# Layer 0 sums taken beside the heads' sums, and layer 0 logits spread by on-chip transfers, in a two-layer graph attention kernel

## The chip, the cores and the metric

The kernel runs on one core of a Trainium2 chip. The core has TensorE (PE, matrix products), VectorE (DVE), ScalarE (ACT), GpSimd (POOL) and SyncE (SP, which here issues nearly all transfers). The metric is device time in microseconds for one execution. All arithmetic is in 32 bit floats.

## The reference

x holds 64 graphs of 256 nodes with 512 features; adj is one 256 x 256 adjacency matrix for all of them. Two attention layers follow one another. Both normalize, clip at zero, attend along the edges and add the result to x.

```python
# layer 0: one head, additive logits
h = relu(layernorm(x))
Wh = h @ W
logits = (Wh @ a_src)[:, :, None] + (Wh @ a_dst)[:, None, :]
logits = where(logits >= 0, logits, 0.2 * logits)
attn = softmax(where(adj == 0, -inf, logits), axis=-1)
x = x + attn @ Wh
# layer 1: eight heads of 64, dot products
h = relu(layernorm(x))
q, k, v = (split_heads(h @ W.T + b) for W, b in ((Wq, bq), (Wk, bk), (Wv, bv)))
attn = softmax(where(adj == 0, -inf, q @ k.T / 8), axis=-1)
x = x + merge_heads(attn @ v) @ Wo.T + bo
```

## The kernel before

**One graph at a time, many graphs in flight.** A graph is 256 tokens, kept as two tiles of 128 partitions (P = 128, NT = NC = 2). The work on a graph is cut into stages, each a Python generator. A loop over i runs a list of steps, `first_half + second_half`; each entry is a stage with an offset, so that one pass works on graphs i - 2 to i + 3. Every engine executes its instructions in the order in which the steps emit them. This hand-written order is the whole schedule. A tile name that is used with one buffer makes its next writer wait for its last reader.

**Short names in the lists.** D0 and N0 are normalize0 (of graphs i + 2 and i + 3), E0 weights0, Q0 quarters0, U0 and US aggregate0, W transform0, N1 and X1 the normalization and transposition of layer 1, K project_qk, V project_v, A and A_OLD attention, AS and AS_OLD scale, O output, BO bias_rows. The large products (K, V, W, O, and the seven small ones of U0) use a Strassen-like scheme of seven half-size products; the sums that it needs (hs, us, as, hq, eq) are made by POOL in `combine`, and DVE adds the products up.

**Layer 0, in order.** normalize0 makes h on ACT and, as its last step (D0), the logits es and ed of the nodes on DVE: four products with accumulation (L511), one column per tile of tokens. weights0 (E0) has three steps. The first spreads es along partitions with two PE transposes into a PSUM bank, pe (L525), from which ACT takes four exponentials (L532, L533). The second takes their maximum on DVE (L537), multiplies it with the mask (em, L540) and adds the two halves up (esum, L542), both on POOL. The third adds esum over partitions with a PE product with ones (ps, L556); DVE clips it (L558) and takes the reciprocal of all 256 columns, the same on all 128 partitions (L559), into the tile rb0. quarters0 (Q0) multiplies em by rb0 on POOL (L578) and makes the differences eq (L588). aggregate0 multiplies h with em (pu, L606).

**Layer 1, the part concerned.** attention takes six steps: the scores of all heads into eight PSUM banks (psc, L838) with exponentials on ACT (L846); four steps of masks and row sums on DVE (L851, L853); and a last step with the products with v (pav, L863) and head_sums. That adds the sums of the eight heads up over partitions with eight PE products on 32-column tiles of the array (psm, L878), so that each head has 16 partitions, and takes one reciprocal of 256 columns (rc, L886). Eight transfers by SP (rb, L909) then spread each head's row over 64 partitions, and scale multiplies aT by rb on DVE (L936) ahead of output. For the last two graphs products with `pick` do it instead of transfers.

**Which graphs.** PLAIN = 3: from graph 3 on, layer 0 goes through quarters0 and the seven small products. PSUM has eight banks, all handed out from one pool by `bank`.

**Around it.** A second path, general, runs only when a test of the weights' size fails; it isn't executed here.

Of the kernel before, what the change touches and what calls it, by code (L numbers as in the profile page):

```python
# [9 lines left out]
F32 = mybir.dt.float32  # L10
# [6 lines left out]
P = 128  # L17
# [6 lines left out]
Q = 32  # L24
# [4 lines left out]
def kernel(  # L29
# [26 lines left out]
    nc = tc.nc  # L56
    B, N, D = x.shape
    NC = N // P
    DC = D // P
    NT = GB * NC  # L60
    TOK = NT * P
    G = B // GB
    DH = D // HEADS
# [16 lines left out]
    ident = const.tile([P, P], F32, tag="ident", name="ident")  # L80
    make_identity(nc, ident)
    ones = const.tile([P, P], F32, tag="ones", name="ones")
# [49 lines left out]
    def bounded():  # L132
        weights = ctx_b.enter_context(tc.tile_pool(name="weights", bufs=1))
        big = ctx_b.enter_context(tc.tile_pool(name="big", bufs=1))
        work = ctx_b.enter_context(tc.tile_pool(name="work", bufs=1))
# [3 lines left out]
        def bank(shape, name):  # L139
            return ps_mm.tile(shape, F32, tag="mm", name=name)  # L140
# [207 lines left out]
        pick = weights.tile([P, P], F32, tag="pick", name="pick")  # L348
# [10 lines left out]
        def constants():  # L359

            ok = weights.tile([P, 2 * DC + 5], F32, tag="ok", name="ok")
            rows = weights.tile([P, 2 * DC], F32, tag="rows", name="rows")
            gms = []
            for n in range(2):
                w_q = whole((wq_sb, wk_sb)[n])  # L370

                gm = work.tile([P, DC, DH], F32, tag="gram", name=f"gram_{n}", bufs=2)
                gms.append(gm)
                for pair in range(2):
                    pg = bank([P, 2, DH], f"pgram_{n}_{pair}")
                    for e in range(2):
                        for c in range(DC):
                            for r in range(2):
                                at = e * P + r * DH
                                wc = w_q[c // 2][pair][:, c % 2, at : at + DH]  # L380
                                nc.tensor.matmul(
                                    pg[r * DH : (r + 1) * DH, e, :], wc, wc,
                                    start=(c == 0), stop=(c == DC - 1),
                                )
                    yield
                    nc.vector.tensor_copy(gm[:, 2 * pair : 2 * pair + 2, :], pg)
                    yield
            for n, gm in enumerate(gms):
                pgs = [bank([P, DC, DH], f"pgram2_{n}_{r}") for r in range(2)]
                for e in range(DC):  # L390
                    for r in range(2):
                        half_p = slice(r * DH, (r + 1) * DH)
                        part = gm[half_p, e, :]
                        nc.tensor.matmul(pgs[r][half_p, e, :], part, part, start=True, stop=True)
                yield
                for e in range(DC):
                    for r in range(2):
                        half_p = slice(r * DH, (r + 1) * DH)
                        ab = work.tile([P, DH], F32, tag="gabs", name=f"gabs_{n}_{e}_{r}")
                        nc.scalar.activation(  # L400
                            ab[half_p], pgs[r][half_p, e, :], AF.Abs,
                            accum_out=rows[half_p, n * DC + e : n * DC + e + 1],
                        )
                yield
            for _ in range(10):
                yield
            sq = weights.tile([P, 4], F32, tag="sq", name="sq")
            for j, col in enumerate((cols["bq"], cols["bk"])):
                junk = work.tile([P, DC], F32, tag="e2", name=f"junk_c_{j}")
                nc.vector.scalar_tensor_tensor(  # L410
                    junk, col, 1.0, col, op0=ALU.mult, op1=ALU.mult, accum_out=sq[:, j : j + 1]
                )
            for _ in range(4):
                yield
            pq = bank([P, 2], "pq")
            nc.tensor.matmul(pq, ones, sq[:, 0:2], start=True, stop=True)
            yield
            nc.vector.tensor_scalar(
                ok[:, 2 * DC + 2 : 2 * DC + 4], pq, 1.0, None, op0=ALU.is_le
            )  # L420
            yield
            for j in range(2):
                junk = work.tile([P, D], F32, tag="e2", name=f"junk_w_{j}")
                nc.vector.scalar_tensor_tensor(
                    junk, wa[j], 1.0, wa[j], op0=ALU.mult, op1=ALU.mult, accum_out=sq[:, 2 + j : 3 + j]
                )
                yield
            nc.vector.tensor_scalar(ok[:, 0 : 2 * DC], rows, 1.0, None, op0=ALU.is_le)
            nc.vector.tensor_scalar(ok[:, 2 * DC : 2 * DC + 2], sq[:, 2:4], 1.95, None, op0=ALU.is_le)
            yield  # L430
            big_v = weights.tile([P, 1], F32, tag="big_v", name="big_v")
            nc.vector.tensor_reduce(big_v, svs, AX.X, ALU.add)
            nc.vector.tensor_scalar(
                ok[:, 2 * DC + 4 : 2 * DC + 5], big_v, 1.0e6, None, op0=ALU.is_le
            )
            okm = weights.tile([P, 1], F32, tag="okm", name="okm")
            nc.vector.tensor_reduce(okm, ok, AX.X, ALU.min)
            for _ in range(12):
                yield
            pk = bank([1, 1], "pok")  # L440
            nc.tensor.matmul(pk, okm, ones[:, 0:1], start=True, stop=True)
            nc.vector.tensor_scalar(flag, pk, P - 0.5, None, op0=ALU.is_lt)
            yield
            picks()
            yield

        class Stats:

# [30 lines left out]
        nodes, edges, sums0, lefts, norms, qkv, vs, outs = {}, {}, {}, {}, {}, {}, {}, {}  # L479

        def normalize0(g):
# [26 lines left out]
            for t in range(NT):  # L508
                for dst, a in ((es, 0), (ed, 1)):
# [3 lines left out]
                        accum_out=dst[:, t : t + 1],  # L513
                    )
            nodes[g] = h, es, ed
            yield

        def weights0(g):

            h, es, ed = nodes[g]  # L520
            edl = small.tile([P, NT], F32, tag="edl", name=f"edl_{g}")
            nc.scalar.mul(edl, ed, NEG_SLOPE)
            pe = bank([P, TOK], f"pe_{g}")
            for t in range(NT):
                nc.tensor.transpose(  # L525
                    pe[:, t * P : (t + 1) * P], es[:, t : t + 1].to_broadcast([P, P]), ident
                )

            e1 = work.tile([P, NC, N], F32, tag="e1", name=f"e1_{g}")
            e2 = work.tile([P, NC, N], F32, tag="e2", name=f"e2_{g}")  # L530
# [10 lines left out]
            esum = work.tile([P, N], F32, tag="esum", name=f"esum_{g}")  # L541
            engine.tensor_tensor(esum, em[:, 0, :], em[:, 1, :], op=ALU.add)  # L542
            edges[g] = [em]
            yield

            if g == 0:
                ps = bank([P, NT], f"ps_{g}")
# [11 lines left out]
            nc.vector.reciprocal(rs, rs)  # L559
            edges[g].append(rs)  # L560
            yield


        PLAIN = 3

        def quarters0(g):

# [257 lines left out]
        def attention(g):  # L825
# [46 lines left out]

            def head_sums():

                psm = bank([P, N], f"psm_{g}")
                for r in range(2):
                    for e in range(DC):
                        nc.tensor.matmul(  # L878
                            psm[e * Q : (e + 1) * Q, :],
                            half[:, r, :],  # L880
                            sums[e][:, r, :],
                            start=(r == 0),
                            stop=(r == 1),
                        )
                rc = work.tile([P, N], F32, tag="rc", name=f"rc_{g}")
                nc.vector.reciprocal(rc, psm)  # L886
                return rc

            exs = [scores(e) for e in range(DC)]
# [14 lines left out]
            if g < G - 2:  # L904
                rb = work.tile([P, DC, N], F32, tag="rb", name=f"rb_{g}")
                for e in range(DC):
                    for r in range(2):
                        src = rc[e * Q + r * (Q // 2) : e * Q + r * (Q // 2) + 1, :]
                        nc.sync.dma_start(  # L909
                            rb[r * DH : (r + 1) * DH, e, :],  # L910
                            bass.AP(
                                tensor=src.tensor, offset=src.offset,
                                ap=[src.ap[0], [0, DH], [1, N]],
                            ),
                        )
            else:

                yield
                rb = [bank([P, N], f"prb_{g}_{e}") for e in range(DC)]
                for e in range(DC):  # L920
                    rows = slice(e * Q, (e + 1) * Q)
                    nc.tensor.matmul(rb[e], pick[rows, :], rc[rows, :], start=True, stop=True)
            outs[g] = aT, rb
            yield

# [89 lines left out]
        def aside(n=1):  # L1015
# [5 lines left out]
        Q0 = (quarters0, 2)  # L1021
# [1 line left out]
        A, A_OLD, BO = (attention, 0), (attention, -1), (bias_rows, 0)  # L1023
        AS, AS_OLD = (scale, -1), (scale, -2)
        first_half = [
            (load, 3), O, D0, K, AS_OLD, O, K, O, K, E0, O, K, E0, O, US, A_OLD, K, O, K, BO, O, K, E0,
        ]
        second_half = [
            A_OLD, A, Q0, A, W, N0, W, W, V, N0, W, W, W, N1, W, N1, A, V, V, V, A, N0, N1, U0, V, AS,
            U0, X1, V, X1, V, X1,  # L1030
        ]

# [259 lines left out]
```

## Time and profile before

| what | value |
|---|---|
| median of 2 runs | 2848.22 us (2846.7 to 2849.74) |
| the profiled execution's own time | 2846.97 us |
| its span, first to last instruction | 2845.2 us |
| PE busy | 2828.9 us (99%) |
| DVE busy | 2473.5 us (87%) |
| POOL busy | 1607.0 us (56%) |
| ACT busy | 1257.3 us (44%) |
| DMA queue of SP | 107.53 MB, 23.7% of 16 engines |
| granted PE clock | 1.00 |

The span is the time between the first and the last instruction of the profiled execution; 1.8 us of its own time lie around it. Busy time is what an engine spends in instructions. PE's records overlap, since its products are pipelined: of two products, the distance between their starts is the price, not the length of one. In a group's line the columns are source line, engine, operation, names out<-in, shapes, count, busy time, mean length in ns, and idle time of the engine ahead of it with what ended it. In a timeline line they are start and length in us, engine, line, operation, names, shapes and count of records that follow one another. A product in 32 bit floats appears as two PE records; a transpose as one.

### The profile page before, as it was taken

The numbers are of one execution on the slowest core, as the hardware profiler recorded it, in microseconds if no ns is written. First come the engines' busy times: TensorE is split into PE (matmuls) and PEld (weight loads), VectorE is DVE, ScalarE is ACT, GpSimd is POOL, SyncE is SP. The second block draws the span as 40 slices with busy tenths as digits, with TensorE's granted clock in tenths as the row PEclk, the third lists the DMA queues.
The fourth block names the chain that finished last, engine by engine and source line by source line (L and its number), as shares of the span: only waits on it lengthen the run. The fifth ranks groups of instructions, "written<-read, shape, count | busy, mean of one in ns | idle before, by whom it ended". The sixth has DMA issues, their size and how long they took to land. (4 is left out here: it accounts for less than half of the span.)

```text
span 2845.2 us, 53317 instructions
## 1 busy us (share of the span) xinstructions
PE 2828.9 (99%) x20316; PEld 2472.3 (87%) x20316; DVE 2473.5 (87%) x3946; ACT 1257.3 (44%) x3045; POOL 1607.0 (56%) x2016
## 2 busy tenths in 40 slices
PE   9999999999999999999999999999999999999998
PEld 6888988988889889888898898888988988889886
DVE  7998988888889888888898888888988888889875
ACT  5444444443444444434444444344454443444532
POOL 2656556566565565665655655656556556565541
PEclk9999999999999999999999999999999999999999
DMA  4122122221221222212212222122122221221221
GB/s 134 23 38 38 34 42 33 36 45 31 38 38 34 42 33 36 45 31 38 39 33 42 33 36 46 31 38 40 32 42 33 36 45 31 38 42 30 34 42 27
DMA packets 82826, 111.01 MB, mean 39 GB/s; under 512 B 11524, under 2 KB 48644, under 8 KB 82566
## 3 DMA queue, kind: packets, MB, share of 16 engines
q1 hardware_dynamic: 82470, 107.53, 23.7%
q8 instruction: 164, 2.69, 0.4%
q14 instruction: 96, 0.79, 0.1%
q0 software_dynamic: 96, 0.01, 0.0%
HBM read 41.43 MB, written 33.55 MB: 26 GB/s over the span
## 5 line engine op out<-in xcount | busy, mean ns | idle before, releaser
L701 DVE TENSOR_TENSOR x<-po,x 128x1024 f32<-128x1024 f32 x875 | 593.8, 685 | 130.2 <-PE po L207 122.9
L851 DVE TENSOR_TENSOR ex<-ex,maskT 128x512 f32<-128x512 f32 x512 | 435.3, 890 | 0.0
L474 POOL TENSOR_SCALAR ve<-ssq 128x2 f32<-128x2 f32 x127 | 25.1, 198 | 483.8 <-ACT h L463 250.6
L846 ACT ACTIVATE ex<-psc 128x512 f32<-128x512 f32 x512 | 257.7, 627 | 89.5 <-PE psc L838 89.4
L871 ACT COPY aT<-pav 128x512 f32<-128x512 f32 x128 | 74.9, 585 | 499.2 <-PE pav L863 468.1
L511 DVE SCALAR_TENSOR_TENSOR junk<-wa,h 128x512 f32<-128x512 f32 x252 | 276.6, 1098 | 7.9 <-ACT h L504 1.1
L216 PEld LDWEIGHTS pqk<-hs,wq_sb 128*128 128x128 f32 x2016 | 264.4, 192 | 12.9
L216 PE MATMUL pqk<-hs,wk_sb 128*128 128x128 f32 x2016 | 266.3, 275 | 0.0
L216 PE MATMUL pqk<-hs,wq_sb 128*128 128x128 f32 x2016 | 265.8, 275 | 0.0
L207 PE MATMUL pv<-wv_sb,hs 128*128 128x256 f32 x1024 | 262.9, 380 | 0.6 <-DVE v L194 0.5
L540 POOL TENSOR_TENSOR em<-e,maskT 128x512 f32<-128x512 f32 x62 | 79.6, 1283 | 321.7 <-DVE e L537 312.0
L207 PE MATMUL po<-wo_sb,as 128*128 128x256 f32 x992 | 255.2, 380 | 0.0
L207 PE MATMUL po<-w_sb,us 128*128 128x256 f32 x1008 | 248.5, 379 | 0.0
L216 PEld LDWEIGHTS pqk<-hs,wk_sb 128*128 128x128 f32 x2016 | 245.4, 192 | 0.0
L838 PE MATMUL psc<-qk 64*128 64x256 f32 x2048 | 239.0, 383 | 0.3 <-DVE rc L886 0.3
L863 PE MATMUL pav<-ex,v 128*64 128x256 f32 x2048 | 235.4, 382 | 0.0
L838 PEld LDWEIGHTS psc<-qk 64*128 64x128 f32 x2048 | 193.1, 187 | 46.9 <-issue 25.0
L165 POOL TENSOR_TENSOR hs<-hT 128x256 f32<-128x256 f32 x64 | 47.0, 735 | 319.2 <-PE pv L207 319.2
L853 DVE TENSOR_TENSOR sm<-ex 128x512 f32<-128x512 f32 x256 | 210.5, 822 | 8.9
L863 PEld LDWEIGHTS pav<-ex,v 128*64 128x64 f32 x2048 | 141.2, 137 | 85.8 <-issue 20.3
L207 PEld LDWEIGHTS po<-w_sb,us 128*128 128x128 f32 x1008 | 191.4, 190 | 26.3 <-DVE x L701 0.3
L216 PEld LDWEIGHTS pqk<-hT,wq_sb 128*128 128x128 f32 x1512 | 198.2, 192 | 9.6
(211 smaller groups left out, 6564.5 us busy)
## 6 DMA issues: line engine op xcount, KB each, us to landing
x<-in_x_dram SPq DMA_DIRECT2D x64, 512.0 KB, 5.6
out_dram<-x SPq DMA_DIRECT2D x128, 256.0 KB, 2.0
rb<-rc SPq DMA_DIRECT2D x496, 64.0 KB, 4.9
wq_sb<-in_L_gnn_Wq_dram SPq DMA_DIRECT2D x4, 256.0 KB, 8.4
wk_sb<-in_L_gnn_Wk_dram SPq DMA_DIRECT2D x4, 256.0 KB, 6.7
w_sb<-in_L_gnn_W_dram SPq DMA_DIRECT2D x4, 256.0 KB, 6.6
wv_sb<-in_L_gnn_Wv_dram SPq DMA_DIRECT2D x4, 256.0 KB, 6.6
wo_sb<-in_L_gnn_Wo_dram SPq DMA_DIRECT2D x4, 256.0 KB, 6.0
```

What stands on the lines that cost most here:

```text
L165: nc.gpsimd.tensor_tensor(s[:, 0], a(1, 0), a(1, 1), op=ALU.add)
L207: nc.tensor.matmul(dst[:, 0:HD], left[:, c, :], wt[:, slot, c, :], start=c == 0, stop=c == 1)
L216: nc.tensor.matmul(dst[:, at : at + P], wt[:, slot, c, e * P : (e + 1) * P], left[:, c, :], start=c == 0, stop=c == 1,)
L511: nc.vector.scalar_tensor_tensor(junk, (wa if g else pas)[a], 1.0, h[:, t, :], op0=ALU.mult, op1=ALU.mult, accum_out=dst[:, t : t + 1],)
L540: engine.tensor_tensor(em, e1, maskT, op=ALU.mult)
L701: nc.vector.tensor_add(dst, src, dst)
L838: nc.tensor.matmul(psc[r][:, m, :], qk[rows, 2 + e % 2, m * P : (m + 1) * P], qk[rows, e % 2, :], start=True, stop=True,)
L846: nc.scalar.activation(ex[:, r, :, :], psc[r], AF.Exp, scale=SCALE)
L851: nc.vector.tensor_mul(ex[:, r, :, :], ex[:, r, :, :], maskT)
L853: nc.vector.tensor_add(sm, ex[:, :, 0, :], ex[:, :, 1, :])
L863: nc.tensor.matmul(pav[r * DH : (r + 1) * DH, i, :], v[j][:, m, at : at + DH], pair[i][:, r, m, :], start=(m == 0), stop=(m == NC - 1),)
L871: nc.scalar.copy(aT[j], pav)
```

## The change

For graphs 3 to 63 two things are done in another way.

The row of logits es isn't transposed by PE. normalize0, in its last step, has SP write the two columns of es into one row of 256 on one partition (es_row, two transfers of 128 single elements), and then spread that row over 128 partitions (es_b). ACT's exponentials read es_b. es_row shares its buffer (tag rc) with the heads' reciprocals, es_b shares esum's.

The sum of esum isn't taken by weights0, whose third step now does nothing there. head_sums of the graph three before takes it, with four PE products of 64 columns each, ahead of its own eight and in the same PSUM bank, which is widened to 320 columns. Each quarter of the nodes lies on 32 partitions, so that the maximum and reciprocal on DVE have 64 columns. Four transfers spread the quarters into rb0, ahead of the eight that spread rb.

The order of the steps changes: the first step of E0 comes after the fourth K instead of the third; the second after the fifth K, with US, BO and A_OLD now ahead of it; the third is dropped. In the second half one V goes ahead of the first U0.

```diff
@@ normalize0
             nodes[g] = h, es, ed
+            if g >= PLAIN:
+                row = work.tile([1, TOK], F32, tag="rc", name=f"es_row_{g}")
+                for t in range(NT):
+                    nc.sync.dma_start(row[:, t * P : (t + 1) * P], es[:, t : t + 1])
+                es_b = work.tile([P, TOK], F32, tag="esum", name=f"es_b_{g}")
+                spread(es_b, row)
+                nodes[g] = h, es_b, ed
             yield
@@ new
+        def spread(dst, row):
+            nc.sync.dma_start(
+                dst,
+                bass.AP(
+                    tensor=row.tensor, offset=row.offset,
+                    ap=[row.ap[0], [0, dst.shape[0]], [1, dst.shape[1]]],
+                ),
+            )
@@ weights0
-            pe = bank([P, TOK], f"pe_{g}")
-            for t in range(NT):
-                nc.tensor.transpose(
-                    pe[:, t * P : (t + 1) * P], es[:, t : t + 1].to_broadcast([P, P]), ident
-                )
+            pe = es
+            if g < PLAIN:
+                pe = bank([P, TOK], f"pe_{g}")
...
             edges[g] = [em]
+            if g >= PLAIN:
+                edges[g].append(esum)
             yield
+            if g >= PLAIN:
+                return
@@ head_sums
-                psm = bank([P, N], f"psm_{g}")
+                psm = bank([P, N + DH], f"psm_{g}")
+                rc = work.tile([P, N + DH], F32, tag="rc", name=f"rc_{g}")
+                g0 = g + PLAIN
+                if g0 < G:
+                    part = slice(N, N + DH)
+                    for e in range(DC):
+                        rows = slice(e * Q, (e + 1) * Q)
+                        nc.tensor.matmul(
+                            psm[rows, part], ones[:, 0:Q], edges[g0][1][:, e * DH : (e + 1) * DH],
+                            start=True, stop=True,
+                        )
...
-                rc = work.tile([P, N], F32, tag="rc", name=f"rc_{g}")
-                nc.vector.reciprocal(rc, psm)
+                if g0 < G:
+                    nc.vector.tensor_scalar_max(rc[:, part], psm[:, part], 1e-38)
+                    nc.vector.reciprocal(rc[:, part], rc[:, part])
+                    rb0 = work.tile([P, N], F32, tag="rb0", name=f"rb0_{g0}")
+                    for e in range(DC):
+                        spread(rb0[:, e * DH : (e + 1) * DH], rc[e * Q : e * Q + 1, part])
+                    edges[g0][1] = rb0
+                nc.vector.reciprocal(rc[:, 0:N], psm[:, 0:N])
@@ order of the steps
-            (load, 3), O, D0, K, AS_OLD, O, K, O, K, E0, O, K, E0, O, US, A_OLD, K, O, K, BO, O, K, E0,
+            (load, 3), O, D0, K, AS_OLD, O, K, O, K, O, K, E0, O, US, BO, A_OLD, K, E0, O, K, O, K,
-            A_OLD, A, Q0, A, W, N0, W, W, V, N0, W, W, W, N1, W, N1, A, V, V, V, A, N0, N1, U0, V, AS,
+            A_OLD, A, Q0, A, W, N0, W, W, V, N0, W, W, W, N1, W, N1, A, V, V, V, A, N0, N1, V, U0, AS,
```

More of the change, by code (lines that the diff above doesn't have):

```diff
@@ L398, in constants @@
                         half_p = slice(r * DH, (r + 1) * DH)
-                        ab = work.tile([P, DH], F32, tag="gabs", name=f"gabs_{n}_{e}_{r}")
+                        ab = work.tile([P, DH], F32, tag="rc", name=f"gabs_{n}_{e}_{r}")
                         nc.scalar.activation(
@@ L445, in constants @@
             yield
+        PLAIN = 3
+        def spread(dst, row):
[6 more added lines that the diff above has]
+            )
         class Stats:
@@ L522, in weights0 @@
             nc.scalar.mul(edl, ed, NEG_SLOPE)
-            pe = bank([P, TOK], f"pe_{g}")
-            for t in range(NT):
-                nc.tensor.transpose(
-                    pe[:, t * P : (t + 1) * P], es[:, t : t + 1].to_broadcast([P, P]), ident
-                )
+            pe = es
+            if g < PLAIN:
+                pe = bank([P, TOK], f"pe_{g}")
+                for t in range(NT):
+                    nc.tensor.transpose(
+                        pe[:, t * P : (t + 1) * P], es[:, t : t + 1].to_broadcast([P, P]), ident
+                    )
             e1 = work.tile([P, NC, N], F32, tag="e1", name=f"e1_{g}")
@@ L561, in weights0 @@
             yield
-        PLAIN = 3
         def quarters0(g):
@@ L873, in head_sums @@
             def head_sums():
-                psm = bank([P, N], f"psm_{g}")
+                psm = bank([P, N + DH], f"psm_{g}")
[8 more added lines that the diff above has]
+                            start=True, stop=True,
+                        )
                 for r in range(2):
@@ L878, in head_sums @@
                         nc.tensor.matmul(
-                            psm[e * Q : (e + 1) * Q, :],
+                            psm[e * Q : (e + 1) * Q, 0:N],
                             half[:, r, :],
@@ L907, in attention @@
                     for r in range(2):
[L908 to L915, printed above, removed]
+                        at = e * Q + r * (Q // 2)
+                        spread(rb[r * DH : (r + 1) * DH, e, :], rc[at : at + 1, 0:N])
             else:
@@ L921, in attention @@
                     rows = slice(e * Q, (e + 1) * Q)
-                    nc.tensor.matmul(rb[e], pick[rows, :], rc[rows, :], start=True, stop=True)
+                    nc.tensor.matmul(rb[e], pick[rows, :], rc[rows, 0:N], start=True, stop=True)
             outs[g] = aT, rb
```

## The prediction

> **What bounds the kernel now.** I read the engine totals first, then TensorE's waits, then the PE, DVE and SP rows of one steady pass of the loop over graphs (43.74 us by the PE rows, 1430.35 to 1474.09), and last the DMA issues.
>
> ```profile
> PE 2828.9 (99%) x20316; PEld 2472.3 (87%) x20316; DVE 2473.5 (87%) x3946; ACT 1257.3 (44%) x3045; POOL 1607.0 (56%) x2016
> ...
> PE pt L750 <- ACT xn L729: 4.9, 3, 3.1
> PE pa L263 <- DMA a_in<-in_L_gnn_a_src_dram: 2.2, 1, 2.2
> PE pwa L274 <- DVE junk_a L270: 1.5, 5, 0.6
> ```
>
> PE is idle for 16.3 us of the 2845.2 us span, and its named waits (3 or 5 times each) lie in the start. In the steady pass it never waits: time is PE work. So an edit pays only by what it takes off PE, and costs only where it makes PE wait.
>
> ```profile
> 1437.40 1.06 PE L216 MATMUL pqk<-hT,wk_sb 128*128 128x128 f32 x8
> 1438.29 0.38 PE L525 MATMUL pe<-ident,es 128*128 128x128 f32 x2
> 1438.51 1.03 PE L207 MATMUL po<-wo_sb,as 128*128 128x256 f32 x4
> ...
> 1449.11 0.60 PE L556 MATMUL ps<-esum,ones 128*128 128x256 f32 x2
> 1449.64 3.67 PE L863 MATMUL pav<-ex,v 128*64 128x256 f32 x32
> 1453.24 1.07 PE L878 MATMUL psm<-sm,half 128*32 128x256 f32 x16
> ```
>
> Columns: start, length, instruction. Lengths overlap, so the price is the distance between starts. The transposes hold PE 0.22 us (1438.29 to 1438.51), the layer 0 sum 0.53 us (1449.11 to 1449.64), the sixteen records of the eight head sums only 1.00 us.
>
> [...] The trace agrees. From the last record of one mode to the first of the next it shows 309 ns where 216 is usual, a drain of 93 ns; and the sixteen 216 ns records of psm fit in 1.00 us, four abreast. [...] In the packet records the first 64 KB spread of rb, all from one partition, moves between 1.12 and 3.27 us after its issue: 30 GB/s. [...] So es_row and es_b cost two latencies in series; no run here shows such a pair yet.
>
> **The change part by part.** It acts on graphs 3 to 63, 61 of 64.
>
> Removed from PE. Two transposes, 2 x 109 = 218 ns. The ones-by-esum product is two records of 216 to 218 ns; the drain before pav (93 ns) stays, since pav then follows a 128-column record, so 434 ns go. Together 0.652 us a graph.
>
> Added to PE. Four matmuls of 64 columns on 32-column tiles, eight records, just ahead of psm in psm's own mode: no second drain. The nearest row is pgram (64 columns, two tiles): 106 ns for its first round after a change of mode, then 58 a round. Two rounds are 0.165 us; psm's first round, now not the first of its mode, falls from 240 to 216 ns. I take 0.14 us. From below: two rounds by columns alone, 2 x 54 - 24 = 0.085. From above: eight records in series at 58, about 0.5.
>
> Net 0.652 - 0.14 = 0.51 us a graph, times 61 = 31 us; with the bounds 0.57 and 0.15, or 35 and 9 us.
>
> DVE. The maximum (411 ns) and reciprocal (1753 ns) of 256 columns go, those of 64 columns come, about 0.22 and 0.5 us by scaling the two rows. 1.4 us a graph less, 89 us in all, worth nothing because DVE isn't the bound. But both now stand ahead of the heads' reciprocal, and the first waits for the whole psm. So the heads' reciprocal, which starts at 1454.38, ends some 0.7 us later, at 1456.9. In the new order the psm bank goes to the second product of transform0, at 1458.87: hidden by 2 us.
>
> DMA and SP. Seven transfers more a graph: two of es_row (128 elements of 4 B), es_b (128 KB), four of rb0 (32 KB each).
>
> ```profile
> 1447.48 2.96 SPq L957 DMA_DIRECT2D out_dram<-x  x2
> 1456.17 6.63 SPq L909 DMA_DIRECT2D rb<-rc  x8
> 1462.84 0.64 SPq L225 DMA_DIRECT2D x<-in_x_dram  x1
> ...
> out_dram<-x SPq DMA_DIRECT2D x128, 256.0 KB, 2.0
> rb<-rc SPq DMA_DIRECT2D x496, 64.0 KB, 4.9
> ```
>
> SP is idle between 1419 and 1447, where es_row and es_b come; behind them wait only the two stores, which have the x buffers as slack.
>
> Chain 1, the logits (own clock of this pass).
>
> ```profile
> 1435.98 1.09 DVE L511 SCALAR_TENSOR_TENSOR junk<-wa,h 128x512 f32<-128x512 f32 x1
> 1443.17 2.51 DVE L851 TENSOR_TENSOR ex<-ex,maskT 128x512 f32<-128x512 f32 x2
> 1445.72 1.10 DVE L853 TENSOR_TENSOR sm<-ex 128x512 f32<-128x512 f32 x1
> ...
> 1442.73 1.27 POOL L540 TENSOR_TENSOR em<-e,maskT 128x512 f32<-128x512 f32 x1 [5.08 <-DVE e L537]
> 1444.08 1.05 POOL L542 TENSOR_TENSOR esum<-em 128x256 f32<-128x256 f32 x1
> ```
>
> The second half of es is ready at 1437.1. es_row then takes 2.0 (the store, also 128 pieces) to 4.9 us (rb's median), I take 2.0. es_b reads twice the bytes of a first rb from one partition: 1.1 + 4.3 + 0.4 = 5.8 us, between 4.9 (the median) and 6.4 (rb's longest). es_b lands at 1445.0, at worst 1448.4. Who waits: ACT's four exponentials (1.57 us) and, behind them on ACT, the copies of the fifth Q/K product; DVE's maximum (0.68), put behind the mask pair that ends near 1446, and behind it six adds; POOL's em and esum (2.4). The sum must be there when PE comes to psm, 1453.24 - 0.65 = 1452.6. Backwards: em by 1450.2, the maximum by 1449.5, es_b by 1447.9. Slack 2.9 us, at worst 0.5 short. Moving us and the bias ahead of em costs nothing: POOL is through with both near 1444.5. The six adds end near 1452, and scores start after 1453.6.
>
> Chain 2, the reciprocals. rb0 is issued from 1455.1, four issues at about 0.6 us[...]. By bytes it lands some 6 us later, 1461; no row shows 256 B pieces, so the upper bound is that its 512 pieces last like rb's 512 of 1 KB: in the packet records the last rb lands 10.9 us after the first issue, 1466. POOL needs 1.4 us for em times rb0 and 1.9 for the two first differences; PE's second pu product, with the V product moved ahead of it, comes at 1468.4. rb0 must land by 1465. Then the eight rb spreads land near 1470 instead of 1467.1; the scaling of aT on DVE, before the next pass's first output product, needs the last by 1473.3. Slack 3 to 4 us in both.
>
> PSUM. Two banks fewer are taken a pass, 48 instead of 50; nothing there comes late.
>
> Sum: 2846.97 (own time of the profiled execution: span 2845.2 plus 1.8) - 31 = 2816. The median of the two runs is 1.3 us above the profiled one, less than the error here.
>
> **The rivals.**
> A. The small matmuls run one after the other. For: no row shows four tiles at 64 columns. Against: psm does four abreast. Net 0.15 us x 61 = 9 us: 2838.
> B. Slower than before: late spreads at rb. Twelve transfers leave one after the other, and O1 stands behind aT on rb. If a 256 B piece costs what a 1 KB piece does, rb0 ends at 1466, and the eight of rb, 9.8 us behind it, at 1475.8: 2.5 us past need, in each pass. PE would wait 2.5 us against 0.51 saved: 2847 + 61 x 2.0 = 2969. It decides from a landing after 1473.8. For: pieces of rb last 46 ns or 500, so they queue. Against: 30 GB/s looks like a limit of bytes, and rb0 carries a quarter of rb's.
> C. No saving: with chain 1 at its upper bounds PE waits 0.5 us at psm, which eats it: 2847. For: the 4 B pieces are new. Against: both latencies must be at their upper end.
> D. Faster by over 2%. Even free sums and no new wait give 0.652 x 61 = 40 us, 2807, and the idle time of the start isn't touched.
>
> **How the numbers follow.** Forecast 0.73, A 0.07, B 0.12 (anywhere from 2848 to 2969, two thirds of it over 2%), C 0.07, D 0.01. The likeliest is 2816. Its own range with the bounds is 2812 to 2838; the range goes to 2808 below, the end of D's arithmetic, and to 2850 above, which takes in A and C and leaves most of B out. 2% is 57 us, about what a measurement of this kernel can tell from no change: faster 0.02, same 0.90, slower 0.08.
>
> **What would show it.** Right: no pe rows and no sum rows on PE but for graphs 0 to 2; starts of the new matmuls and of the first psm record 0.14 to 0.19 us apart; a pass of 43.2 us; PE idle still near 16 us. Chain 1 is wrong if psm waits for POOL's esum, chain 2 if pu waits for POOL or po for DVE's aT. The forecast is wrong if PE's idle time grows by more than 10 us.

## The result and the profile after

| | before | after |
|---|---|---|
| median | 2848.22 us (2846.7 to 2849.74) | 2821.36 us (2820.66 to 2822.05) |
| profiled execution, own time | 2846.97 us | 2820.66 us |
| its span | 2845.2 us | 2818.9 us |
| a steady pass, distance of the starts of psm | 43.746 us | 43.205 us |
| PE idle, span minus busy | 16.3 us | 19.8 us |

The ratio after to before is 0.9903 with the interval [0.988, 0.9927]: about 1% less time, within the 2% that was called no change, and 5 us above the forecast of 2816. The steady pass gained 0.541 us; 61 passes of that are 33.0 us. The two profiled executions differ by only 26.3 us. So the pass did slightly better than forecast, and 6.7 us were lost somewhere else. Most of this section is about where.

First the engine totals of the kernel after:

```profile
PE 2799.1 (99%) x20560; PEld 2455.8 (87%) x20560; DVE 2335.3 (83%) x3946; ACT 1259.0 (45%) x3045; POOL 1502.0 (53%) x2016
```

Some of its groups (count, busy time and mean in ns, then the idle time before them and what ended it):

```profile
L876 DVE TENSOR_TENSOR ex<-ex,maskT 128x512 f32<-128x512 f32 x512 | 368.0, 759 | 0.0
L603 POOL TENSOR_TENSOR em<-em,rb 128x256 f32<-128x256 f32 x122 | 86.2, 728 | 468.7 <-DMA rb<-rc 468.7
L555 ACT ACTIVATE e<-es_b,ed 128x256 f32<-128x256 f32 x122 | 61.0, 500 | 433.9 <-DMA es_b<-es_row 433.9
```

And three of its DMA issues (count, KB each, median us from issue to landing):

```profile
es_b<-es_row SPq DMA_DIRECT2D x61, 128.0 KB, 6.4
rb<-rc SPq DMA_DIRECT2D x244, 32.0 KB, 3.8
es_row<-es SPq DMA_DIRECT2D x122, 0.5 KB, 1.9
```

PE is still busy 99% of the span. ACT and POOL now wait more than 430 us each for the new transfers (7 to 8 us a pass), and PE doesn't notice: neither engine is the bound. Those two large idle figures cost nothing, because PE's own list of waits has neither of them (total, number of times, longest):

```profile
PE pt L775 <- ACT xn L754: 4.9, 3, 3.1
PE psc L863 <- DVE qk L201: 3.3, 1, 3.3
PE pa L263 <- DMA a_in<-in_L_gnn_a_src_dram: 2.3, 1, 2.3
PE pav L888 <- ACT gabs L400: 2.0, 1, 2.0
```

The first and third were there before. The second and fourth are new, and each happens once. No wait happens 61 times: the pass runs without a stall, as before. PE's rows of one steady pass, around the added matmuls:

```profile
1400.72 0.32 PE L908 MATMUL psm<-esum,ones 128*32 128x64 f32 x8
1400.86 1.05 PE L914 MATMUL psm<-sm,half 128*32 128x256 f32 x16
1401.84 3.72 PE L863 MATMUL psc<-qk 64*128 64x256 f32 x32
...
1439.34 1.06 PE L216 MATMUL pqk<-hs,wk_sb 128*128 128x128 f32 x8
1440.33 3.67 PE L888 MATMUL pav<-ex,v 128*64 128x256 f32 x32
```

Before, pav followed the two ps records; now it follows a Q/K product directly. The heads' sums start 0.14 us after the small matmuls.

**The start is where the 6.7 us went.** The first head sums, before and then after:

```profile
95.58 1.07 PE L878 MATMUL psm<-sm,half 128*32 128x256 f32 x16
98.78 1.05 PE L914 MATMUL psm<-sm,half 128*32 128x256 f32 x16
```

They start 3.2 us later. The second ones come 44.98 us behind them before and 48.48 us after: 3.5 us. Together these two account for the loss. The rows of the kernel after in that stretch (start, length, engine and line; in brackets the idle time before it and what ended it):

```profile
90.22 0.22 ACT L400 ACTIVATE gabs<-pgram 64x64 f32<-64x64 f32 x1 [9.21 <-DMA es_b<-es_row]
...
93.36 5.36 PE L888 MATMUL pav<-ex,v 128*64 128x256 f32 x32 [2.00 <-ACT gabs L400]
99.18 1.14 ACT L823 ACTIVATE p<-pqk,bias 128x128 f32<-128x128 f32 x4
100.35 0.89 DVE L198 TENSOR_TENSOR qk<-qk,p 128x512 f32<-128x512 f32 x1 [3.97 <-ACT p L823]
103.12 1.13 PE L863 MATMUL psc<-qk 64*128 64x256 f32 x8 [3.30 <-DVE qk L201]
```

gabs is scratch of the test of the weights' size, which is made once, in the first passes of the loop. An edit that the diff above leaves out moves it into the buffer rc:

```diff
-                        ab = work.tile([P, DH], F32, tag="gabs", name=f"gabs_{n}_{e}_{r}")
+                        ab = work.tile([P, DH], F32, tag="rc", name=f"gabs_{n}_{e}_{r}")
```

es_row lies in rc too, and rc is one buffer. So the first gabs has to wait until the transfer that spreads es_row has read it, and ACT stands for 9.21 us; what its program has behind that gabs comes late with it. The sixteen gabs start between 80.2 and 88.5 us before, and between 90.2 and 98.7 us after. PE waits 2.00 us at pav, and the profile names gabs, which reads its products from PSUM, as what ended the wait. Behind the last gabs ACT gets to p, the summand of a Q/K product (99.18); DVE waits 3.97 us for it, and PE 3.30 us at psc for DVE's sum.

The 5.3 us of stalls are not the whole price. The table by windows has for the stretch 60 to 110 us (length, then busy time of PE, PEld, DVE, ACT and POOL with counts, then granted PE clock, DMA share, GB/s), first before,

```profile
60.00:110.00 50.00, 45.96 (x332) 38.42 (x331) 47.02 (x68) 29.00 (x88) 27.99 (x33) 1.00 0.15 11
```

then after:

```profile
60.00:110.00 50.00, 41.45 (x298) 34.40 (x297) 40.47 (x59) 23.84 (x72) 23.01 (x24) 0.90 0.14 7
```

The granted clock falls from 1.00 to 0.90: three windows of 3.41 us at half clock lie there, from 73.6, 94.0 and 104.3 us. The profiled execution of the kernel before has none in the start. The first window follows a stall of 3.1 us at pt that both kernels have. The other two follow the two new stalls, and in them pav takes 5.36 us, where 3.67 is usual, and psc 5.41, where 3.72 is usual. So the 6.7 us have two parts: 3.5 us are more idle time of PE (19.8 against 16.3 us), and 3.2 us are longer records (PE is busy for 2799.1 us, where 2828.9 - 33.0 = 2795.9 would be left).

### The profile page after: what moved, and what is told of

Same layout as the page of the kernel before. It is cut to its first block, busy times and chain, and to the rows that moved or that the text cites. A ratio compares the mean times of both kernels' runs of the same rounds, so it can differ in the third digit from the quotient of the medians.

```text
span 2818.9 us, 54598 instructions
## 1 busy us (share of the span) xinstructions
PE 2799.1 (99%) x20560; PEld 2455.8 (87%) x20560; DVE 2335.3 (83%) x3946; ACT 1259.0 (45%) x3045; POOL 1502.0 (53%) x2016
## 5 line engine op out<-in xcount | busy, mean ns | idle before, releaser
L876 DVE TENSOR_TENSOR ex<-ex,maskT 128x512 f32<-128x512 f32 x512 | 368.0, 759 | 0.0
L603 POOL TENSOR_TENSOR em<-em,rb 128x256 f32<-128x256 f32 x122 | 86.2, 728 | 468.7 <-DMA rb<-rc 468.7
L555 ACT ACTIVATE e<-es_b,ed 128x256 f32<-128x256 f32 x122 | 61.0, 500 | 433.9 <-DMA es_b<-es_row 433.9
L207 PE MATMUL pv<-wv_sb,hs 128*128 128x256 f32 x1024 | 253.5, 380 | 0.6 <-DVE v L194 0.5
L563 POOL TENSOR_TENSOR em<-e,maskT 128x512 f32<-128x512 f32 x62 | 79.2, 1278 | 263.8 <-DVE e L560 254.0
L207 PEld LDWEIGHTS pv<-wv_sb,hs 128*128 128x128 f32 x1024 | 190.2, 191 | 24.5 <-DVE v L194 0.9
```

The source lines that it names most:

```text
L207: nc.tensor.matmul(dst[:, 0:HD], left[:, c, :], wt[:, slot, c, :], start=c == 0, stop=c == 1)
L555: nc.scalar.activation(e1[:, m, :], pe, AF.Exp, bias=ed[:, m : m + 1])
L563: engine.tensor_tensor(em, e1, maskT, op=ALU.mult)
L603: nc.gpsimd.tensor_tensor(em[:, m, :], em[:, m, :], rb, op=ALU.mult)
L876: nc.vector.tensor_mul(ex[:, r, :, :], ex[:, r, :, :], maskT)
```

## The experiments

Where nothing else is said, an experiment starts from the version with gabs in another buffer, so that the start disturbs no comparison. Its pass is also 43.205 us.

**The change again** (no edit).

> The changed kernel once more, beside its variants. Both theories: 0.9905 of before, 2821 us; one pass of the loop over graphs 43.20 us against 43.75; the start some 7 us longer than before's.

Measured: 2820.27 us (2819.7 to 2823.28), ratio 0.9904 [0.9888, 0.9919]; pass 43.205 us. The first result stands.

**gabs in another buffer.**

```diff
-                        ab = work.tile([P, DH], F32, tag="rc", name=f"gabs_{n}_{e}_{r}")
+                        ab = work.tile([P, DH], F32, tag="s2v", name=f"gabs_{n}_{e}_{r}")
```

> The changed kernel with gabs in the buffer s2v instead of rc. Theory G (the 5 us missing from the forecast are lost at the start, because gabs shares rc with es_row and so makes ACT wait for the landing of es_b): ACT's wait of 9.2 us ahead of gabs, PE's waits of 2.0 us at pav and 3.3 us at psc and the windows of half PE clock that follow them go, 7 us less, 2814 us; the pass stays 43.20 us. Theory S (the loss comes from the order of steps and the transfers themselves, whatever buffer gabs has): the waits move to the exponentials and stay, 2821 us.

Measured: 2816.35 us (2815.08 to 2818.73), ratio 0.9893 [0.9878, 0.9908]. Repeated later:

> The kernel with gabs apart once more, beside it: 2816 us, 0.989 of before; its profile again without half clock in the start, or[...] with one or two.

Measured: 2817.44 us (2816.07 to 2818.82), ratio 0.9894 [0.9877, 0.991]. The highest of all these runs (2818.8) lies below the lowest of the change's in the repetition (2819.7), though the intervals of the ratios overlap. The gain is 4 us, where theory G expected 7. The waits for gabs and for the late Q/K sum are gone from PE's list; one new wait is left in the first pass, and here is the start of that version: its first psm row,

```profile
97.80 0.32 PE L908 MATMUL psm<-esum,ones 128*32 128x64 f32 x8 [2.73 <-POOL esum L565]
```

and its window:

```profile
60.00:110.00 50.00, 43.79 (x328) 36.80 (x327) 46.00 (x66) 27.33 (x83) 26.68 (x31) 1.00 0.20 12
```

The clock is 1.00 here, and PE does 328 records in the stretch against 298. So the buffer of gabs costs about 4 us. In the repetition the same kernel had the same stalls, but also two windows of 3.4 us at half clock in its start, and its span was 3.0 us longer (2816.3 against 2813.3 us). So these windows vary between executions, and I don't count them as caused by gabs alone. Of the 6.7 us about 4 are shown to hang on this edit. The wait for esum doesn't make up the rest: the execution without half clock has this wait too, and its span is 31.9 us below that of before, only 1.1 us short of the 33.0 us that the passes gain. What is missing beyond that goes with the half clock.

**Move what fills ACT and DVE in the start, to let that esum come earlier.** In the first pass DVE also combines the weights (combine_w). This version spreads one of these combinations over four later places:

```diff
-        def combine_w(wt):
-            for to, a, b in ((T1, T3, B11), (T2, B22, T1), (T3, B22, T3), (T4N, B21, T2)):
+        def combine_w(wt, part=slice(0, 4)):
+            for to, a, b in ((T1, T3, B11), (T2, B22, T1), (T3, B22, T3), (T4N, B21, T2))[part]:
...
-                if i == 1 and n == 9:
-                    combine_w(wo_sb)
+                if i == 1 and n in (24, 28, 32, 36):
+                    combine_w(wo_sb, slice(n // 4 - 6, n // 4 - 5))
```

> As the kernel with gabs apart, with DVE's four subtractions for the quarters of wo_sb, which stand ahead of the fourth mask in pass 1 and last 5.2 us there, put one by one into the second half of that pass. Theory (they make DVE late for the maximum, POOL for esum, and PE waits 2.7 us for it at psm in pass 1): that wait goes, 3 us less than the kernel with gabs apart, 2813 us. Rival (the subtractions cost DVE the same in the second half, where PE waits for its adds): 2816 us or more.

Measured: 2816.95 us (2816.41 to 2820.2), ratio 0.9892 [0.9876, 0.9909]: no gain over the 2817.44 us of the version with gabs apart that ran beside it. The wait for esum is gone, and PE's list has instead

```profile
PE psc L863 <- DVE qk L201: 2.7, 1, 2.7
```

A stall of the same size one product further on: in the start, taking away the wait that ends last brings up the next. The two versions can't be told apart by their times.

**The logits by transposes again, the sums as in the change.**

```diff
-            if g >= PLAIN:
-                row = work.tile([1, TOK], F32, tag="rc", name=f"es_row_{g}")
...
-                nodes[g] = h, es_b, ed
...
-            pe = es
-            if g < PLAIN:
-                pe = bank([P, TOK], f"pe_{g}")
-                for t in range(NT):
...
+            pe = bank([P, TOK], f"pe_{g}")
+            for t in range(NT):
...
```

> As the kernel with gabs apart, but the row of logits comes from the two PE transposes again; es_row and es_b are gone, the sums stay beside the heads' sums. If the price of a PE record is the distance between starts: 0.218 us a pass more, 61 x 0.218 = 13 us above the kernel with gabs apart, 2827 us, pass 43.42 us. Rival: transposes were free beside other PE work, then no difference.

Measured: 2832.27 us (2830.77 to 2832.97), ratio 0.9946 [0.9933, 0.996]; pass 43.423 us. That is 0.218 us above 43.205, the price forecast for two transposes. It divides the gain of a pass: the transfers in place of transposes are worth 0.218 us, the sums beside the heads' sums 43.746 - 43.423 = 0.323 us. In the first pass PE waits for esum here too:

```profile
PE psm L898 <- POOL esum L555: 3.1, 1, 3.1
```

No transfer stands in the path of this esum. So that wait doesn't come from the transfers; by the version with combine_w spread out, where it is gone, it comes from DVE's work in the first pass.

**The small matmuls three times.**

```diff
-                    for e in range(DC):
+                    for e in [*range(DC)] * 3:
```

> As the kernel with gabs apart, with the four small matmuls issued three times over in each pass instead of once. Theory of the forecast (four tiles abreast, 58 ns a round of four): two more sets are four rounds, 0.23 us a pass, 61 x 0.23 = 14 us, 2830 us, pass 43.44 us. Rival (one after the other): sixteen more records at 58 ns, 0.93 us a pass, 57 us, 2873 us.

Measured: 2831.16 us (2829.51 to 2832.2), ratio 0.9937 [0.9924, 0.9951]; pass 43.428 us. Its rows:

```profile
1404.44 0.54 PE L908 MATMUL psm<-esum,ones 128*32 128x64 f32 x24
1404.80 1.05 PE L914 MATMUL psm<-sm,half 128*32 128x256 f32 x16
```

24 records take 0.36 us to the start of psm, where 8 took 0.14. Two more sets cost 0.223 us, and a set is two rounds of records, so a round of four tiles costs 0.223 / 4 = 56 ns, and one record costs no more than a quarter of that. Single starts within a round lie 6 to 7 ns apart, and the next round begins 37 ns later. Had the tiles run in series, two sets would have cost 16 records of 56 ns, 0.9 us.

**The sum of 256 columns, in the place of the small matmuls.** One product with ones where the four were; DVE's maximum and reciprocal have 256 columns and write rb0, and its four transfers go.

```diff
-                    for e in range(DC):
-                        rows = slice(e * Q, (e + 1) * Q)
-                        nc.tensor.matmul(
-                            psm[rows, part], ones[:, 0:Q], edges[g0][1][:, e * DH : (e + 1) * DH],
-                            start=True, stop=True,
-                        )
+                    ps = bank([P, N], f"ps_{g0}")
+                    nc.tensor.matmul(ps, ones, edges[g0][1], start=True, stop=True)
...
-                    nc.vector.tensor_scalar_max(rc[:, part], psm[:, part], 1e-38)
-                    nc.vector.reciprocal(rc[:, part], rc[:, part])
-                    for e in range(DC):
-                        spread(rb0[:, e * DH : (e + 1) * DH], rc[e * Q : e * Q + 1, part])
+                    nc.vector.tensor_scalar_max(rb0, ps, 1e-38)
+                    nc.vector.reciprocal(rb0, rb0)
```

> As the kernel with gabs apart, but layer 0's sum is the product of 256 columns with ones again, with DVE over 256 columns, no rb0 spreads, at the place of the four small matmuls, between pav and psm. If the kernel with the sums apart lost its 120 us by the place of the sum (ahead of pav, where esum isn't there yet), not by its kind: no wait at ps; 0.43 us for the product, 0.09 us for one more change of mode, 0.12 us less for the small ones, 0.41 us a pass, 25 us, 2841 us, pass 43.62 us. Rival (the loss is in the kind: DVE's longer reciprocals, a ninth bank): above 2900 us.

Measured: 2850.78 us (2847.01 to 2853.18), ratio 1.0007 [0.9998, 1.0015]; pass 43.722 us, 0.517 above 43.205. No wait happens in the steady pass. Its PE rows:

```profile
1454.63 3.67 PE L888 MATMUL pav<-ex,v 128*64 128x256 f32 x32
1458.24 0.70 PE L907 MATMUL ps<-esum,ones 128*128 128x256 f32 x2
1458.87 1.07 PE L910 MATMUL psm<-sm,half 128*32 128x256 f32 x16
```

ps to psm is 0.63 us. It sits between two products in other modes of the array, so there is one change of mode more. The prediction's 309 ns at a change of mode, where 216 is usual, accounts for 93 ns; what I had not counted is that the two records of ps start 320 ns apart, not 216. The account closes: 0.434 (two records, as forecast) + 0.093 + 0.104 - 0.113 (the small matmuls, net, from the gaps given below) = 0.518 us, against 0.517 measured. In this place the sum eats nearly all of the transposes' gain too (the pass is 0.024 us shorter than before's); it is the small tiles, not the later place, that make it cheap.

**The sum of 256 columns in its old step.** The third step of E0 and its product are back, in the new order, and head_sums takes no sum.

```diff
-            if g >= PLAIN:
-                edges[g].append(esum)
...
-            if g >= PLAIN:
-                return
...
-                if g0 < G:
+                if False:
...
-            (load, 3), O, D0, K, AS_OLD, O, K, O, K, O, K, E0, O, US, BO, A_OLD, K, E0, O, K, O, K,
+            (load, 3), O, D0, K, AS_OLD, O, K, O, K, O, K, E0, O, US, BO, A_OLD, K, E0, O, K, O, K, E0,
```

> As the kernel with gabs apart, but layer 0's sums are taken by the product of 256 columns with ones again, with its own bank, and by DVE over 256 columns; the logits still come by es_row and es_b. 0.434 us a pass back and 0.14 us of the four small matmuls gone: 0.29 us, 61 x 0.29 = 18 us above the kernel with gabs apart, 2832 us, pass 43.49 us. Rival (the small matmuls cost as much as eight records in series, 0.5 us): no worse, or faster by 4 us, than the kernel with gabs apart.

Measured: 2942.85 us (2940.34 to 2948.41), ratio 1.0339 [1.0324, 1.0353]. A miss by 110 us, and it taught the most. The mean steady pass is 45.24 us, the median 44.68; PE's list and a row of it:

```profile
PE ps L579 <- POOL esum L565: 76.6, 61, 7.3
...
1420.86 0.70 PE L579 MATMUL ps<-esum,ones 128*128 128x256 f32 x2 [0.87 <-POOL esum L565]
```

There is the wait that the change could have had. In the old place ps stands ahead of pav, 3.6 us earlier on PE than psm. With the logits by transfer, esum isn't there yet. Windows of half clock lie along the run too, 12 of 3.41 us. The previous experiment had the same product 3.6 us later and no stall: 2942.85 against 2850.78, 92 us for the place, although the later place pays for one change of mode more. So the late logits and the late sum belong together: the transfers may take their 8.5 us (median of 61 passes of the kernel after, from es to the first exponential) only because the sum moved behind pav.

**The old order of the first half, the rest as in the change** (without the dropped third E0).

```diff
-            (load, 3), O, D0, K, AS_OLD, O, K, O, K, O, K, E0, O, US, BO, A_OLD, K, E0, O, K, O, K,
+            (load, 3), O, D0, K, AS_OLD, O, K, O, K, E0, O, K, E0, O, US, A_OLD, K, O, K, BO, O, K,
```

> As the kernel with gabs apart, with the steps of the first half in the order of the kernel before (the exponentials after the third K, their maximum ahead of the fourth mask, us and bias behind), without its last E0. DVE would wait at the maximum for the landing of es_b, with the fourth mask and six adds behind it: PE waits 1.5 to 2 us at psm or psc in each pass, some 2926 us. Rival (the order is worth nothing, the slack of chain 1 holds in both): 2816 us.

Measured: 2892.05 us (2884.33 to 2892.31), ratio 1.0153 [1.0137, 1.0168]; the median pass is 44.10 us. The list of waits has for DVE and for PE

```profile
DVE e L560 <- ACT e L556: 301.1, 63, 6.1
...
PE psc L863 <- DVE qk L201: 59.7, 61, 3.0
```

and the rows are

```profile
1468.46 0.69 DVE L560 TENSOR_TENSOR e<-e,e 128x512 f32<-128x512 f32 x1 [4.82 <-ACT e L556]
1476.41 3.72 PE L863 MATMUL psc<-qk 64*128 64x256 f32 x32 [0.82 <-DVE qk L201]
```

DVE's maximum stands in its queue and waits 4.8 us for exponentials whose logits are still under way. The Q/K adds behind it come late, and PE waits for them at psc. The stall on DVE is 4.8 us and on PE about 1 us (59.7 / 61), where 1.5 to 2 were expected: DVE had most of it to spare. In the kernel after, with the new order, DVE waits there for 91.0 us in 62 times, 1.5 us each, against 301.1 us in 63; the order is worth 2892.05 - 2816.35 = 76 us, more than twice what the change gains.

**rb0's spreads behind those of rb.** The four transfers of rb0 are issued after the eight of rb instead of ahead of them.

```diff
-                    for e in range(DC):
-                        spread(rb0[:, e * DH : (e + 1) * DH], rc[e * Q : e * Q + 1, part])
...
+                g0 = g + PLAIN
+                if g0 < G:
+                    for e in range(DC):
+                        spread(
+                            edges[g0][1][:, e * DH : (e + 1) * DH],
+                            rc[e * Q : e * Q + 1, N : N + DH],
+                        )
```

> As the kernel with gabs apart, but the four spreads of rb0 are issued behind the eight of rb. rb's eight need 10.9 us from issue to the last landing, so that rb0 lands some 15 us after the reciprocals instead of 6. If chain 2 has 5 us of slack at the second pu product: PE waits some 4 us in each pass, 2816 + 61 x 4 = 3060 us, and the waits are at pu, for POOL. Rival (POOL's wait for rb0 is hidden in any order): 2816 us.

Measured: 3247.93 us (3244.8 to 3248.89), ratio 1.1398 [1.1381, 1.1416]. PE's list:

```profile
PE pu L631 <- POOL em L603: 175.8, 61, 3.5
PE pu L631 <- POOL eq L613: 46.3, 61, 1.8
PE pt L775 <- ACT uT L642: 28.7, 37, 1.1
```

a pass by rows,

```profile
1426.27 1.41 POOL L603 TENSOR_TENSOR em<-em,rb 128x256 f32<-128x256 f32 x2 [16.79 <-DMA rb<-rc]
1427.05 0.71 PE L631 MATMUL pu<-em,h 128*128 128x128 f32 x4 [2.83 <-POOL em L603]
```

and one by its window:

```profile
1408.82:1459.07 50.25, 45.70 (x330) 40.01 (x332) 36.12 (x61) 19.50 (x47) 23.40 (x33) 0.97 0.32 38
```

rb0 now lands 13.7 us after the first issue of rb instead of 6.2 after its own, and PE waits in every pass. The direction was expected, the size wasn't: the pass is 7.0 us longer, of which the named waits are (175.8 + 46.3 + 28.7) / 61 = 4.1. The other 2.9 us are longer records: PE is busy for 2978.2 us, against 2796.1 in the version with gabs apart, 3.0 us more a pass. Most of that fits the clock. The trace has 63 stretches of half clock before its end, 320.9 us together or 94 windows of 3.41 us; half of that time is 160 us, at most 2.6 us a pass (an estimate from the trace's clock). No run took the clock's part away.

## Why the prediction was right, and where it was wrong

**PE work alone counts: right for the pass.** Forecast 0.51 us a pass, measured 0.541. The DVE work that went was 138 us, and none of it shows in the time.

**The terms on PE.**

| step | forecast, us | measured, us |
|---|---|---|
| two transposes | 0.218 | 0.218 |
| ps without the 93 ns of a change of mode | 0.434 | 0.436 (0.323 + 0.113) |
| small matmuls, net | 0.14 (0.085 to 0.5) | 0.113 |
| sum | 0.51 | 0.541, by the pass |

The mis-sized term is the small matmuls. Eight starts give gaps of 7, 7, 7, 60, 7, 6, 6 and 37 ns, 0.137 us together; the first round of the heads' sums then takes 216 ns instead of 240, so 0.113 net. The row of ps has no measurement of its own: it is what the 0.323 us of the experiment with the transposes leave when the small matmuls' price is added. The prediction used the round after a change of mode of pgram, 106 ns; this one took 7 + 7 + 7 + 60 = 81. At 64 columns four records start within 21 ns and the next round 60 ns later, and in the run with the small matmuls three times a round of four cost 56 ns. So these tiles work beside one another, and rival A is out.

**DVE: sizes right or nearly, worth nothing as said.** In the rows of the pass,

```profile
1401.97 0.22 DVE L923 TENSOR_SCALAR rc<-psm 128x64 f32<-128x64 f32 x1 [1.86 <-PE psm L914]
1402.23 0.55 DVE L924 RECIPROCAL rc<-rc 128x64 f32<-128x64 f32 x1
1402.70 1.70 DVE L929 RECIPROCAL rc<-psm 128x256 f32<-128x256 f32 x1
```

the maximum has 0.22 us (forecast 0.22) and the reciprocal 0.55 (0.5), so the heads' reciprocal comes 0.73 us later (0.7). Missed: DVE lost 138 us where 89 were forecast. The mask products fell from 435.3 to 368.0 us and the row sums sm from 210.5 to 177.5, while one of the Q/K adds (L198) rose from 43.6 to 85.2. With the old order these are back at 435.8, 227.2 and 43.0 us, so it is the order of the steps. The rows show what runs beside POOL's em and esum. Before, it is the two mask products of the prediction's chain 1, 2.51 us beside L540 and L542. Two others, with neither beside them, take half of that, and the add L198 comes after both:

```profile
1421.70 1.28 DVE L851 TENSOR_TENSOR ex<-ex,maskT 128x512 f32<-128x512 f32 x2
1447.34 0.68 DVE L198 TENSOR_TENSOR qk<-qk,p 128x512 f32<-128x512 f32 x1
```

After, L198 runs beside em (L563, 1439.85 to 1441.12) and takes twice its length before:

```profile
1440.28 1.38 DVE L198 TENSOR_TENSOR qk<-qk,p 128x512 f32<-128x512 f32 x1
```

An add with one operand in PSUM (L201) kept its length, 675 ns before and after. POOL's busy time in all is no measure of this: it is 1607.0 us before, 1502.0 after and 1697.6 with the old order, but 1484.2 with the sum in its old step, where the mask products took 383.0. By what means the one engine lengthens the other's instructions was not shown.

**Chain 1, the logits: right.** The rows of one pass, with SP's:

```profile
1425.48 2.79 SPq L533 DMA_DIRECT2D es_row<-es  x2
1427.65 0.08 DVE L524 DVE_READ_ACCUMULATOR junk<-wa,h 128x1 f32 x1
1430.81 0.53 SPq L452 DMA_DIRECT2D es_b<-es_row  x1
1437.27 0.51 ACT L555 ACTIVATE e<-es_b,ed 128x256 f32<-128x256 f32 x1 [8.17 <-DMA es_b<-es_row]
1439.08 0.69 DVE L560 TENSOR_TENSOR e<-e,e 128x512 f32<-128x512 f32 x1 [2.44 <-ACT e L556]
1439.85 1.27 POOL L563 TENSOR_TENSOR em<-e,maskT 128x512 f32<-128x512 f32 x1 [5.08 <-DVE e L560]
1441.19 1.05 POOL L565 TENSOR_TENSOR esum<-em 128x256 f32<-128x256 f32 x1
```

From es (1427.73) to the issue of es_b are 3.1 us here, where 2.0 were taken: the second es_row is issued at 1427.75, and its last landing comes 3.0 us later, where the median is 1.9 and the longest 3.4. SP issues es_b 0.08 us behind that landing. Over the 61 passes the median from es to the issue of es_b is 2.05 us. From there to ACT's start are 6.5 us (5.8 taken, 6.4 the upper end). ACT starts 9.5 us after es in this pass and 8.5 in the median, where 7.9 were taken. esum ends at 1442.24 and PE needs it at 1443.93: slack 1.7 us here, one of five passes behind the first with 1.5 to 1.9; the median is 2.7, forecast 2.9. Rival C, a stall at psm, didn't come in the steady passes, but the old step for the sum was already a loss. The two latencies stand in series, as taken, and the price is 8.5 us.

**Chain 2, the reciprocals: right.**

```profile
1402.87 9.79 SPq L452 DMA_DIRECT2D rb<-rc  x12
1409.09 1.41 POOL L603 TENSOR_TENSOR em<-em,rb 128x256 f32<-128x256 f32 x2 [7.72 <-DMA rb<-rc]
1410.99 0.46 POOL L613 TENSOR_TENSOR eq<-em,eq 128x128 f32<-128x128 f32 x1
1416.40 0.61 PE L631 MATMUL pu<-eq,hq 128*128 128x128 f32 x4
```

The first issue is at 1402.87 and POOL starts at 1409.09: 6.2 us, where some 6 were taken from the bytes and 10.9 was the bound by pieces. The second difference ends at 1411.45, and PE comes at 1416.40: slack 5.0 us (3 to 4 forecast). Scaling aT on DVE doesn't wait for rb. So rival B didn't happen: in the packet records rb0's 512 pieces of 256 B move within 4.5 us, where rb's 512 of 1 KB took 9.4 us in the pass of before. A late rb0 does cost time, though: issued eight transfers later, it cost 432 us.

**The start: wrong.** The step that failed is "PE idle still near 16 us", and behind it an edit that the prediction didn't price at all: the buffer of gabs. PE's idle time measured 19.8 us. The prediction also has no term for the clock, and 3.2 us of longer records came on top. I had listed the waits of the start and looked only at whether the change takes them away, not at whether the one buffer of rc, with es_row as a new user and gabs moved in, makes ACT wait in the first pass. Of the 6.7 us, about 4 hang on gabs. The rest is the 1.1 us that the version with gabs apart still lacks without half clock, and windows of half clock, which differ from one execution to the next. The 6.7 us, less the 2 us by which the passes did better, are the difference between the 31 us forecast and the 26.3 measured. So it is partly luck that the total came so close: an error in the pass made up for part of the error in the start.

## What to carry to other kernels

Transfers of 8.5 us in place of 0.2 us of PE pay when PE is the bound and the consumer can be moved behind other work; move the consumer first, and read its slack from the passes, since here the same transfers with the old order or the old place of the sum cost 76 to 126 us. Small reductions belong next to a product that is already in the same mode of the array: four 64-column sums cost 0.11 us there, where one 256-column sum in the same place costs 0.63. Follow every buffer that a diff shares anew, also one that is used only in the first pass: here ACT's wait of 9.21 us for one was followed by waits of 3.97 us on DVE and of 2.00 and 3.30 us on PE.

## What the runs showed of the hardware beside this

- A change of mode cost more than the 93 ns ahead of it (309 ns where 216 is usual). After it, the two 256-column records of ps were 320 ns apart instead of 216: 0.197 us for one extra change. Where the heads' sums came second in their mode, their first round took 216 instead of 240 ns.
- PE fell to half clock in windows of 3.41 us after stalls of 2.0 to 3.3 us (in the start of the kernel after, with its stall of 3.1 us at pt). The stretches of full clock between its three windows are 17.07 and 6.83 us long, five times and twice 3.413. Half clock doesn't follow such a stall each time. The stall of 3.1 us at pt, around 73 us, stands in the lists of all twelve profiled executions; in the kernel after half clock begins within 1 us of its end, in the kernel before and in the first execution with gabs apart (clock 1.00 from 60 to 110 us) it doesn't. So the price of such a stall varies from one execution to the next.
- A transfer that spreads one partition over 128 took 6.4 us for 128 KB (the median of 61); four that spread 32 KB each, from four partitions, were through 6.2 us after the first was issued, in the pass of chain 2.
